# Gate and up of a pair of expert tiles: seven block products, with partial sums kept in PSUM, in place of eight

## The chip, the cores and the metric

The kernel runs on one core of a Trainium2 chip. The metric is the device time of one execution in microseconds (us), as the median of the runs shown. All data are float32 unless a line says otherwise. The engines are named as in the profile: PE is TensorE (PEld its weight loads), DVE is VectorE, ACT is ScalarE, POOL is GpSimd, and SP issues most DMAs. P is 128, D is 512, KC (the number of 128-row chunks of D) is 4.

## What is computed

The reference is a decoder of two layers over 16 sequences of 128 tokens: a state space scan, cross attention, a ternary feed forward, self attention, gated cross attention, and last a mixture of experts. The change touches only the last, which for a token x reads (cut):

```python
scores = softmax(x @ gate_w.T)                 # 64 experts in 8 groups of 8
topk_w, topk_idx = top_k(scores, 8)
flat = w_e[:, inv_map]; scalar = flat.sum(-1)  # weight of each group
soft = softmax(where(flat == 0, -1e9, flat))
xg = x[:, None, :] + einsum('ngi,ghi->ngh', soft, mask_up_w)
g = einsum('ngh,gih->ngi', xg, gate_proj_w)    # 352 x 512 for each group
u = einsum('ngh,gih->ngi', xg, up_proj_w)
a = silu(g) * u
d = einsum('ngi,ghi->ngh', a, down_proj_w)
y = einsum('ng,ngh->nh', scalar, d)
```

## The kernel before

The stages run one after the other; `stage_moe` is the last, from about 2150 us of the profiled span to its end. A token is copied into the bucket of each group that it needs, and the groups then work on tiles of 128 tokens. The work list `units` holds 53 units, 40 of two tiles ("pairs") and 13 of one. It goes through the eight groups twice: first the first five tiles of each group (two pairs and a single), then the later ones (mostly three pairs); near the end four `beyond` units for overfull buckets stand between the groups, and the last pair takes its tokens from `placed`. Each of the 16 passes (`q`) has its weights: `gu`, 128 x 4 x 704, which holds in its columns 256 rows of gate, 256 of up, and the remaining 96 of gate and 96 of up; and `dn` for down.

The loop in `stage_moe` is a software pipeline written out by hand. In step t it does, for PE, in this order: `rest` (L2010) of unit t, the 96 + 96 left-over columns with the tokens as stationary operand, into PSUM tile `pr`; `gate` (L2035), 8 matmuls into `pg`, and after them the transposes of the left-over activations (`pta`, L2041); `up` (L2045), 8 matmuls into `pu`; then `places` of unit t+2 (transposes, `pts`, L1985); `turn_in` of unit t+1, which makes that unit's token block `xgT` (soft times mask-up plus the transposed row, PSUM tiles `px`, copied out by ACT at L2007 and DVE at L2007); and last `down` of unit t (`y`, L2063), whose results DVE scales (`yo`, L2080) and ACT's queue stores (L2081). A float32 matmul of the source appears as two records of the profile, so 8 matmuls are "x16".

The element work between them: ACT takes silu of `pr` (L2020) and DVE multiplies it with the up part (L2021) before `pta` can start; ACT copies `pta` to `aT` (L2043); ACT takes silu of `pg` (L2038), DVE multiplies `pu` into it (L2047), and both `aT` and `act` are read by `down`.

PSUM has eight banks: `pg`, `pu` and `pr` have one tile each (pool `s6g`), the pool `s6p` has three tiles that all of `pta`, `pts` and the two `px` take in turn, and `y` has two. The matmuls of `gate`, `up`, `down`, `places` and `turn_in` are kept in program order; the order of everything else on each engine's queue is the tile scheduler's. Each engine runs its own queue in order.

`half()` in each step also moves other work along: the routing of the last eight token blocks (`route`, L1691, in the first nine steps or so; its exponentials change ACT's function table, which silu changes back), the gathers of finished results (`got`, L2086), POOL's additions of them to x (L2098), and layer norms.

Of the kernel before, what the change touches and what calls it, by code (L numbers as in the profile page):

```python
# [10 lines left out]
F32 = mybir.dt.float32  # L11
# [4 lines left out]
AF = mybir.ActivationFunctionType  # L16
ALU = mybir.AluOpType
# [3 lines left out]
P = 128  # L21
NB = 16
D = 512
KC = D // P
# [1573 lines left out]
class Moe:  # L1598
# [330 lines left out]
    def pair(self, g, j, n):  # L1929

        u, k = Ctx(), self.k
        u.g, u.j, u.n, u.s = g, j, n, None
# [6 lines left out]
    def placed(self, g, b, n):  # L1939

        u = Ctx()
        u.g, u.n, u.b, u.to, u.s = g, n, b, None, None
        u.src = [self.k.rows[b + i][:, :].unsqueeze(1) for i in range(n)]
        return u

    def beyond(self, s):

        u = Ctx()
        u.s, u.n, u.to = s, 1, [self.k.over_results[s][1:, :]]
        return u  # L1950

    def fetch(self, u):
# [7 lines left out]

    def open(self):

        self.wk = self.k.moe_ctx.enter_context(self.k.tc.tile_pool(name="s6o", bufs=1, side="right"))
        self.depth = 1
        self.opened = u = self.pair(0, 0, 2)
        self.fetch(u)
        yield
        yield
        self.places(u)
        yield  # L1970
        yield from self.turn_in(u)
# [17 lines left out]
    def turn_in(self, u, keep=lambda ins: ins):  # L1989

        nc, n, mup = self.nc, u.n, self.mup[u.g] if u.s is None else self.over_mup[u.s]
        u.xT = self.wk.tile([P, KC, 2, P], F32, tag="xgT", name="xgT")
        pxs = [self.pp.tile([P, 2, 2, P], F32, tag="pp", name="px") for _ in range(2)]
        cols = [slice(c * P, (c + 1) * P) for c in range(KC)]
        for c, at in enumerate(cols):
            keep(nc.tensor.matmul(
                pxs[c // 2][:, c % 2, 0:n], mup[:, at], u.soft[:, 0:n], start=c % 2 == 0, stop=False, skip_group_check=True
            ))
        for h, px in enumerate(pxs):
            for e in range(2):  # L2000
                for i in range(n):
                    keep(nc.tensor.matmul(
                        px[:, e, i], u.row[:, i, cols[2 * h + e]], self.k.ident, is_transpose=True,
                        start=False, stop=e == 1 and i == n - 1, skip_group_check=True,
                    ))
            copy = nc.vector.tensor_copy if h else nc.scalar.copy
            copy(u.xT[:, 2 * h : 2 * h + 2, 0:n], px[:, :, 0:n])  # L2007
            yield

    def rest(self, u):  # L2010

        nc, n, R, (gu, _) = self.nc, u.n, self.I - 2 * P, u.w
        pr = self.pgu.tile([P, 2, 2 * R], F32, tag="pr", name="pr")
        for i in range(n):
            for c in range(KC):
                nc.tensor.matmul(pr[:, i], u.xT[:, c, i], gu[:, c, 4 * P :], start=c == 0, stop=c == KC - 1)  # L2016
        u.rest = self.rests[0]
        self.rests.reverse()
        r = u.rest[:, 0:n, 0:R]
        nc.scalar.activation(r, pr[:, 0:n, 0:R], AF.Silu)  # L2020
        nc.vector.tensor_tensor(r, pr[:, 0:n, R:], r, ALU.mult)  # L2021

    def whole(self, u, lo, tag):

        n, (gu, _) = u.n, u.w
        ps = self.pgu.tile([P, 2, 2, P], F32, tag=tag, name=tag)
        for e in range(2):
            for c in range(KC):
                at = lo + e * P
                self.k.tc.keep_in_program_order(  # L2030
                    self.nc.tensor.matmul(ps[:, e, 0:n], gu[:, c, at : at + P], u.xT[:, c, 0:n], start=c == 0, stop=c == KC - 1)  # L2031
                )
        return ps[:, :, 0:n]

    def gate(self, u):  # L2035
        pg = self.whole(u, 0, "pg")
        u.aT = self.wk.tile([P, 2, 2, P], F32, tag="act", name="act")
        self.nc.scalar.activation(u.aT[:, :, 0 : u.n], pg, AF.Silu)  # L2038
        pt = self.pp.tile([P, 2, P], F32, tag="pp", name="pta")
        for i in range(u.n):  # L2040
            self.k.tc.keep_in_program_order(self.nc.tensor.transpose(pt[:, i], u.rest[:, i], self.k.ident))  # L2041
        u.rT = self.wk.tile([P, 2, P], F32, tag="aT", name="aT")
        self.nc.scalar.copy(u.rT[:, 0 : u.n], pt[:, 0 : u.n])  # L2043
# [112 lines left out]
def stage_moe(k):  # L2156
# [4 lines left out]
    with ExitStack() as ctx:  # L2161
# [120 lines left out]
        with tc.If(over > 0):  # L2282
            for b in range(NB):
                nc.sync.dma_start(k.x[b], k.rows[b][:, 0:D])
            for g in range(NG):
                w = m.load(wp, g)
                for b in range(0, NB, 2):
                    u = m.placed(g, b, 2)
                    u.w = w
                    m.fetch(u)  # L2290
                    m.places(u)
# [147 lines left out]
```

## Time and profile before

| what | value |
|---|---|
| three runs | 2970.22, 2973.87, 2977.48 us (median 2973.87) |
| the profiled execution | 2971.48 us, of which the span of its trace 2969.5 us |
| from 2150 to 2970 us of the span (820 us) | PE busy 797.0, PEld 616.8, DVE 252.1, ACT 152.4, POOL 426.5 us |
| all POOL additions of gathered results (L2098) | 134 x 1.27 us |
| all DVE multiplications after up (L2047) | 40 of 128 x 512 at 0.691 us, 13 of 128 x 256 at 0.423 us |
| granted TensorE clock, mean of the execution | 0.991 |

A row of a timeline gives start, duration, engine, source line, operation, output from inputs, shape and count; several like instructions are merged into one row. The duration of a PE row runs to the modelled end of its last matmul; the time that PE spends on a row is read from its start to the start of the next one.

### The profile page before, as it was taken

To read this page: it belongs to the slowest core of one execution; us is meant where nothing else is said; L and a number is where in the kernel's file an instruction comes from. 1 tells how busy PE (TensorE), PEld (TensorE's weight loads), DVE (VectorE), ACT (ScalarE), POOL (GpSimd) and SP (SyncE) were. 2 spreads that over 40 slices of the span, in tenths; PEclk is the share of its full clock that TensorE was granted. 3 is DMA by queue.
4 is the path that set the end of the run, shared out by engine and by line. 5 is a ranking of instruction groups with operands and counts; after the bars stand their busy time and mean duration, and the time that the engine had idled before them with its cause. 6 is when DMAs were issued, how large, how long until landed. Compare 5 with 4: busy or idle time off the path is not lost.

```text
span 2969.5 us, 41833 instructions
## 1 busy us (share of the span) xinstructions
PE 2868.5 (97%) x14422; PEld 1929.5 (65%) x14446; DVE 1887.1 (64%) x4263; ACT 1326.2 (45%) x3265; POOL 1562.8 (53%) x1352
## 2 busy tenths in 40 slices
PE   7999999999999999999999999999999999999998
PEld 6666665555555555555787656566577777777776
DVE  6999997766766676755897798667743321332224
ACT  6887884333343333336434698655632211111111
POOL 7999996434333333431333474246646564335555
PEclk9999999999999999999999999999999999999999
DMA  6755454780000000005000200224267776555664
GB/s 201 217 138 128 130 134 124 261 301 15 8 8 15 8 8 15 8 29 159 27 1 1 72 2 1 61 87 150 95 223 250 249 240 203 172 190 169 203 206 145
DMA packets 177393, 345.24 MB, mean 116 GB/s; under 512 B 25277, under 2 KB 84157, under 8 KB 175638
## 3 DMA queue, kind: packets, MB, share of 16 engines
q1 hardware_dynamic: 126342, 217.64, 24.4%
q0 software_dynamic: 26016, 80.80, 8.1%
q10 hardware_dynamic: 24816, 44.05, 4.0%
q8 instruction: 116, 1.90, 0.3%
q14 instruction: 103, 0.84, 0.1%
HBM read 256.22 MB, written 151.99 MB: 137 GB/s over the span
## 4 chain that ended last, share of the span: by engine, by line
PE 65%; DVE 13%; ACT 3%; issue 1%; POOL 1%; DMA 1%; SPq 0%; ACTq 0%; DVEq 0%; POOLq 0%
PE y L2063 8%; PE pq L708 7%; PE po L828 6%; PE pu L2031 5%; PE pg L2031 5%; PE pr L2016 4%; PE po L1040 4%; PE ao L817 3%; PE sc L777 3%; PE pt L568 2%; PE pg L1020 2%; PE pT L805 2%; PE pu L1020 2%; PE pk L708 1%; PE pw L1514 1%
## 5 line engine op out<-in xcount | busy, mean ns | idle before, releaser
L797 POOL TENSOR_TENSOR pr<-pr,sm 128x512 f32<-128x512 f32 x128 | 135.3, 1057 | 366.2 <-DVE sm L796 276.5
L66 POOL TENSOR_TENSOR dBx<-dtx,BC 128x1024 f32<-128x1024 f32 (+1 forms) x131 | 300.5, 2316 | 16.0 <-DVE h L66 9.4
L790 ACT ACTIVATE pr<-sc,mx,sf 128x256 f32<-128x256 f32 x256 | 142.3, 560 | 335.7 <-DVE mx L783 299.7
L66 ACT ACTIVATE h<-dt,negA 128x254 f32<-128x254 f32 x512 | 244.1, 477 | 16.8 <-ACT h L66 0.2
L2086 POOL DMA_INDIRECT got<-results,gidx x126 | 121.1, 961 | 215.6 <-DMA results<-yo 184.6
L828 PE MATMUL po<-w,aT 128*128 128x512 f32 x512 | 233.1, 593 | 1.0 <-DVE aT L822 1.0
L708 PE MATMUL pq<-w,xT 128*128 128x512 f32 x512 | 231.4, 595 | 0.0
L2098 POOL TENSOR_TENSOR x<-got,x 128x512 f32<-128x512 f32 x134 | 168.2, 1272 | 89.0 <-DMA got<-results,gidx 86.1
L679 POOL TENSOR_TENSOR m<-m,m 128x512 f32<-128x512 f32 x96 | 122.6, 1277 | 116.6 <-DVE m L674 113.3
L66 DVE TENSOR_TENSOR_SCAN h<-h,dBx 128x1024 f32<-128x1024 f32 x72 | 164.9, 2290 | 27.1 <-ACT h L66 21.5
L2047 DVE TENSOR_TENSOR act<-pu,act 128x512 f32<-128x512 f32 (+1 forms) x53 | 33.1, 625 | 230.5 <-PE pu L2031 209.2
L2063 PE MATMUL y<-dn,act 128*128 128x512 f32 x372 | 175.2, 593 | 1.5 <-DVE act L2047 1.5
L2031 PE MATMUL pu<-xgT,gu 128*128 128x256 f32 (+1 forms) x848 | 172.2, 357 | 0.0
L2031 PE MATMUL pg<-xgT,gu 128*128 128x256 f32 (+1 forms) x848 | 170.0, 354 | 0.0
L66 PE MATMUL pkv<-w,cT 128*128 128x512 f32 x368 | 167.5, 598 | 1.1 <-DMA w<-in_x_wvT 1.1
L1030 POOL TENSOR_TENSOR lo<-sg,hi 128x512 fp32r<-128x512 f32 x64 | 84.1, 1314 | 156.5 <-ACT hi L1029 156.4
L2080 DVE TENSOR_SCALAR yo<-y,row 128x512 f32<-128x512 f32 x87 | 65.3, 751 | 155.0 <-PE y L2063 153.2
L708 PEld LDWEIGHTS pq<-w,xT 128*128 128x128 f32 x512 | 94.6, 191 | 101.0 <-issue 93.3
L828 PEld LDWEIGHTS po<-w,aT 128*128 128x128 f32 x512 | 94.7, 190 | 100.9 <-issue 97.0
L1830 POOL DMA_INDIRECT bucket<-r_row,r_to x126 | 124.8, 990 | 58.8 <-issue 35.7
L2031 PEld LDWEIGHTS pg<-xgT,gu 128*128 128x128 f32 x848 | 145.5, 191 | 14.4
L2031 PEld LDWEIGHTS pu<-xgT,gu 128*128 128x128 f32 x848 | 144.1, 192 | 15.0
(462 smaller groups left out, 6962.4 us busy)
## 6 DMA issues: line engine op xcount, KB each, us to landing
bucket<-zeros SPq DMA_DIRECT2D x88, 388.0 KB, 9.1
BC<-bcd SPq DMA_DIRECT2D x128, 256.0 KB, 5.4
row<-bucket SPq DMA_DIRECT2D x39, 776.0 KB, 5.3
gu<-in_moe_guT SPq DMA_DIRECT2D x16, 1408.0 KB, 7.8
results<-yo ACTq DMA_DIRECT2D x87, 256.0 KB, 4.5
x_k<-kv ACTq DMA_DIRECT2D x32, 256.0 KB, 4.2
x_v<-kv ACTq DMA_DIRECT2D x32, 256.0 KB, 5.1
v<-x_v SPq DMA_DIRECT2D x32, 256.0 KB, 2.6
```

What stands on the lines that cost most here:

```text
L66: return self.tc.keep_in_program_order(call(*args, **kw))
L679: nc.gpsimd.tensor_tensor(m1, m1, m2, ALU.add)
L708: nc.tensor.matmul(ps, src[:, c], w[c], start=c == 0, stop=c == KC - 1)
L790: nc.scalar.activation(pr[:, j], st.sc[g, i][:, j], AF.Exp, scale=st.sf[:, h : h + 1], bias=st.mx[g, i][:, j : j + 1], accum_out=sm[:, j : ...
L797: nc.gpsimd.tensor_tensor(pr, pr, sm.unsqueeze(2).to_broadcast([P, 2, 2 * P]), ALU.mult)
L828: nc.tensor.matmul(st.po, aT[:, j], k.wo[h // 8][:, h % 8], start=h == 0, stop=h == G * J - 1)
L1020: nc.tensor.matmul(p[:, e], w[:, c, at : at + P], sn.qT[:, :, c], start=c == 0, stop=c == KC - 1)
L1830: return self.nc.gpsimd.indirect_dma_start(out=table[:, :], out_offset=bass.IndirectOffsetOnAxis(ap=to[:, i, g : g + 1], axis=0), in_=row[ ...
L2031: self.nc.tensor.matmul(ps[:, e, 0:n], gu[:, c, at : at + P], u.xT[:, c, 0:n], start=c == 0, stop=c == KC - 1)
L2063: self.k.tc.keep_in_program_order(self.nc.tensor.matmul(y, aT, dn[:, c], start=c == 2, stop=c == 1))
L2086: self.nc.gpsimd.indirect_dma_start(out=got[:, :], out_offset=None, in_=table, in_offset=bass.IndirectOffsetOnAxis(ap=at, axis=0),)
L2098: self.nc.gpsimd.tensor_tensor(self.k.x[b], got, self.k.x[b], ALU.add)
```

## The change

For every pair except the first one of the stage (and except the overflow path, which is not taken with these inputs), gate and up together are taken as one product of 2 x 2 blocks. The left matrix has gate and up (256 rows each) as its block rows and the two halves of D as its block columns; the right matrix has the halves of D as block rows and the two tiles of tokens as block columns. The eight block products become seven, by Strassen's scheme in Winograd's form. A block product is 4 matmuls of 128 x 128 by 128 columns (two row blocks, two chunks of D).

- `weight_sums` makes four sums of weight blocks for each pass, 128 x 512 each, on DVE; three live in the slot of the tile `row` of an older pool, the fourth in a tile of its own.
- `differences` makes four differences of token blocks, 128 x 256 each, on DVE, after the copies of `turn_in`.
- `split_gate` runs products 1, 2, 5, 6, 3 before `rest`; product 7 stands inside `rest`, between the matmuls of the first and the second tile; product 4 stands in `split_last`, where `up` was.
- Partial sums stay in PSUM: product 6 is added on top of product 1 (`u.q`, in the tile `pu`), 7 and 4 on top of that, product 3 on top of product 5 (in the tile `pg`). Between two products ACT copies the value that is needed at that point (L2055, L2058, L2059), and DVE adds (L2060, L2062, L2069) and multiplies (L2070, L2074).
- silu of the 512 gate columns reads SBUF (L2063) instead of PSUM.
- The transposes `pta` move from behind `gate` to behind product 4 (`turn_rest`).
- `xgT` has one buffer instead of two.

```diff
     def turn_in(self, u, keep=lambda ins: ins):
-        u.xT = self.wk.tile([P, KC, 2, P], F32, tag="xgT", name="xgT")
+        u.xT = self.wk.tile([P, KC, 2, P], F32, tag="xgT", name="xgT", bufs=1)
...
+        if u.split:
+            self.differences(u)
+
+    def weight_sums(self, pool, gu):
+        nc = self.nc
+        (a11, a12), (a21, a22) = [[gu[:, 2 * h : 2 * h + 2, r : r + 2 * P] for h in range(2)] for r in (0, 2 * P)]
+        s4 = pool.tile([P, 2, 2 * P], F32, tag="sums", name="sums", bufs=1)
+        s = self.left.tile([P, 2, self.ROW], F32, tag="row", name="sums3").rearrange("p a b -> p (a b)")
+        s1, s2, s3 = (s[:, 4 * P * i : 4 * P * (i + 1)].rearrange("p (c r) -> p c r", c=2) for i in range(3))
+        for to, x, y, op in (
+            (s1, a21, a22, ALU.add), (s2, s1, a11, ALU.subtract), (s3, a11, a21, ALU.subtract), (s4, a12, s2, ALU.subtract)
+        ):
+            nc.vector.tensor_tensor(to, x, y, op)
+        return a11, a12, s4, a22, s1, s2, s3
+
+    def differences(self, u):
+        (b11, b12), (b21, b22) = [[u.xT[:, 2 * h : 2 * h + 2, i] for i in range(2)] for h in range(2)]
+        t = self.left.tile([P, KC, 2, P], F32, tag="xgT", name="diff")
+        for i, (x, y) in enumerate(((b12, b11), (b22, t[:, 0]), (b22, b12), (b21, t[:, 1]))):
+            self.nc.vector.tensor_tensor(t[:, i], x, y, ALU.subtract)
+        u.right = b11, b21, b22, t[:, 3], t[:, 0], t[:, 1], t[:, 2]
+
+    def seventh(self, u, n, ps, start=False):
+        w, x = u.w[2][n - 1], u.right[n - 1]
+        for e in range(2):
+            for c in range(2):
+                self.k.tc.keep_in_program_order(self.nc.tensor.matmul(
+                    ps[:, e], w[:, c, e * P : (e + 1) * P], x[:, c], start=start and e == 0 and c == 0, stop=c == 1,
+                    skip_group_check=True,
+                ))
+
+    def split_gate(self, u):
+        nc = self.nc
+        gate = self.pgu.tile([P, 2, 2, P], F32, tag="pg", name="pg")
+        u.q = self.pgu.tile([P, 2, 2, P], F32, tag="pu", name="pu")[:, 0]
+        x, r = gate[:, 0], gate[:, 1]
+        u.fifth = self.wk.tile([P, 2, P], F32, tag="fifth", name="fifth", bufs=1)
+        u.aT = self.wk.tile([P, 2, 2, P], F32, tag="act", name="act")
+        a, b = u.aT[:, :, 0], u.aT[:, :, 1]
+        self.seventh(u, 1, u.q, start=True)
+        self.seventh(u, 2, x, start=True)
+        nc.scalar.copy(a, u.q)
+        self.seventh(u, 5, r)
+        self.seventh(u, 6, u.q)
+        nc.scalar.copy(u.fifth, r)
+        nc.scalar.copy(b, u.q)
+        nc.vector.tensor_tensor(a, x, a, ALU.add)
+        self.seventh(u, 3, r)
+        nc.vector.tensor_tensor(b, r, b, ALU.add)
+        nc.scalar.activation(u.aT, u.aT, AF.Silu)
+
+    def split_up(self, u):
+        nc = self.nc
+        self.seventh(u, 7, u.q)
+        nc.vector.tensor_tensor(u.fifth, u.q, u.fifth, ALU.add)
+        nc.vector.tensor_tensor(u.aT[:, :, 1], u.fifth, u.aT[:, :, 1], ALU.mult)
+
+    def split_last(self, u):
+        self.seventh(u, 4, u.q)
+        self.nc.vector.tensor_tensor(u.aT[:, :, 0], u.q, u.aT[:, :, 0], ALU.mult)
...
     def rest(self, u):
...
+            if u.split and not i:
+                self.split_up(u)
...
@@ stage_moe, step t @@
-                m.rest(u)
-                m.gate(u)
+                if u.split:
+                    m.split_gate(u)
+                    m.rest(u)
+                else:
+                    m.rest(u)
+                    m.gate(u)
             half()
             m.tick()
             if u:
-                m.up(u)
+                if u.split:
+                    m.split_last(u)
+                    m.turn_rest(u)
+                else:
+                    m.up(u)
+            if t + 1 in first and t > 0:
+                q = first[t + 1]
+                weights[q] = *weights[q], m.weight_sums(wp, weights[q][0])
...
             if u:
                 m.down(u)
                 m.store(u)
+            if t == 0:
+                weights[0] = *weights[0], m.weight_sums(wp, weights[0][0])
```

More of the change, by code (lines that the diff above doesn't have):

```diff
@@ L1931, in pair @@
         u, k = Ctx(), self.k
-        u.g, u.j, u.n, u.s = g, j, n, None
+        u.g, u.j, u.n, u.s, u.split = g, j, n, None, n == 2
         late = j >= self.FIRST
@@ L1937, in pair, with placed @@
         return u
-    def placed(self, g, b, n):
+    def placed(self, g, b, n, split=True):
         u = Ctx()
-        u.g, u.n, u.b, u.to, u.s = g, n, b, None, None
+        u.g, u.n, u.b, u.to, u.s, u.split = g, n, b, None, None, split
         u.src = [self.k.rows[b + i][:, :].unsqueeze(1) for i in range(n)]
@@ L1948, in beyond @@
         u = Ctx()
-        u.s, u.n, u.to = s, 1, [self.k.over_results[s][1:, :]]
+        u.s, u.n, u.split, u.to = s, 1, False, [self.k.over_results[s][1:, :]]
         return u
@@ L1961, in open @@
     def open(self):
-        self.wk = self.k.moe_ctx.enter_context(self.k.tc.tile_pool(name="s6o", bufs=1, side="right"))
+        self.wk = self.left = self.k.moe_ctx.enter_context(self.k.tc.tile_pool(name="s6o", bufs=1, side="right"))
         self.depth = 1
         self.opened = u = self.pair(0, 0, 2)
+        u.split = False
         self.fetch(u)
@@ L2010, in rest @@
+    def split_up(self, u):
[6 more added lines that the diff above has]
+        self.nc.vector.tensor_tensor(u.aT[:, :, 0], u.q, u.aT[:, :, 0], ALU.mult)
     def rest(self, u):
-        nc, n, R, (gu, _) = self.nc, u.n, self.I - 2 * P, u.w
+        nc, n, R, gu = self.nc, u.n, self.I - 2 * P, u.w[0]
@@ L2015, in rest @@
             for c in range(KC):
-                nc.tensor.matmul(pr[:, i], u.xT[:, c, i], gu[:, c, 4 * P :], start=c == 0, stop=c == KC - 1)
+                self.k.tc.keep_in_program_order(
+                    nc.tensor.matmul(pr[:, i], u.xT[:, c, i], gu[:, c, 4 * P :], start=c == 0, stop=c == KC - 1)
+                )
+            if u.split and not i:
+                self.split_up(u)
         u.rest = self.rests[0]
@@ L2023, in whole @@
     def whole(self, u, lo, tag):
-        n, (gu, _) = u.n, u.w
+        n, gu = u.n, u.w[0]
         ps = self.pgu.tile([P, 2, 2, P], F32, tag=tag, name=tag)
@@ L2038, in gate, with turn_rest @@
         self.nc.scalar.activation(u.aT[:, :, 0 : u.n], pg, AF.Silu)
+        self.turn_rest(u)
+    def turn_rest(self, u):
         pt = self.pp.tile([P, 2, P], F32, tag="pp", name="pta")
@@ L2287, in stage_moe @@
                 for b in range(0, NB, 2):
-                    u = m.placed(g, b, 2)
+                    u = m.placed(g, b, 2, split=False)
                     u.w = w
```

## The prediction

> **What bounds the kernel now.** First the page's busy times and its chain of waits, then the busy times by stretch of the expert stage, then the timeline of one pair.
>
> ```profile
> PE 2868.5 (97%) x14422; PEld 1929.5 (65%) x14446; DVE 1887.1 (64%) x4263; ACT 1326.2 (45%) x3265; POOL 1562.8 (53%) x1352
> ...
> PE 65%; DVE 13%; ACT 3%; issue 1%; POOL 1%; DMA 1%; SPq 0%; ACTq 0%; DVEq 0%; POOLq 0%
> ...
> 2400.00:2560.00 160.00, 160.00 (x790) 125.00 (x790) 31.50 (x52) 21.73 (x56) 73.79 (x70) 1.00 0.59 193
> ```
>
> From 2400 to 2560 us PE is busy for all of 160 us, at clock 1.00, while DVE works 31.5 and ACT 21.7. What leaves PE's queue shortens the stage; what DVE or ACT gets costs nothing until PE waits for it. PE in one pair:
>
> ```profile
> 2566.75 2.76 PE L2016 MATMUL pr<-gu,xgT 128*128 128x192 f32 x16
> 2569.35 3.62 PE L2031 MATMUL pg<-xgT,gu 128*128 128x256 f32 x16
> 2572.80 0.38 PE L2041 MATMUL pta<-ident,rest 128*128 128x128 f32 x2
> 2573.02 3.62 PE L2031 MATMUL pu<-xgT,gu 128*128 128x256 f32 x16
> 2576.48 0.38 PE L1985 MATMUL pts<-ident,row 128*128 128x128 f32 x2
> 2576.61 0.72 PE L1996 MATMUL px<-soft,mup 128*128 128x256 f32 x4
> 2577.17 1.04 PE L2002 MATMUL px<-ident,row 128*128 128x128 f32 x8
> 2578.04 1.02 PE L2063 MATMUL y<-dn,aT 128*128 128x512 f32 x2
> ...
> 2583.20 2.11 PE L2016 MATMUL pr<-gu,xgT 128*128 128x192 f32 x12
> ```
>
> From start to start: 16.45 us for the pair, of it 2.60 `pr`, 3.45 `pg`, 3.46 `pu`, 0.22 `pta`, 0.13 `pts`, 0.56 + 0.87 `px`, 5.16 `y`, and no gap. The elementwise work hides because each result has 3.45 us of other matmuls before PE needs it:
>
> ```profile
> 2569.55 0.33 ACT L2020 ACTIVATE rest<-pr 128x192 f32<-128x192 f32 x1 [7.55 <-PE pr L2016]
> 2569.91 0.36 DVE L2021 TENSOR_TENSOR rest<-pr,rest 128x192 f32<-128x192 f32 x1 [2.21 <-ACT rest L2020]
> ```
>
> `rest` is done at 2570.27 and `pta` wants it at 2572.80. These rows also give hops: PE's row ends at 2569.35, ACT begins 0.20 later; ACT to DVE 0.03.
>
> **The saving.** 32 records of 256 columns (6.91 us) become 56 of 128 columns. Units of one tile show what such a record costs:
>
> ```profile
> 2253.07 1.95 PE L2031 MATMUL pu<-xgT,gu 128*128 128x128 f32 x16
> 2254.86 0.38 PE L1985 MATMUL pts<-ident,row 128*128 128x128 f32 x2
> ```
>
> 16 in 1.79 us, 0.112 each, so 56 take 6.27 and a pair saves 0.64: an eighth off, less 3.6% for the smaller matmuls. 40 pairs less the first are 39: -25.0 us.
>
> **The new waits in each pair.** Two places come too close. The remaining hops are in a unit where `pta` already waited:
>
> ```profile
> 2219.23 0.35 DVE L2021 TENSOR_TENSOR rest<-pr,rest 128x192 f32<-128x192 f32 x1
> 2219.64 0.44 PE L2041 MATMUL pta<-ident,rest 128*128 128x128 f32 x2 [0.20 <-DVE rest L2021]
> 2219.91 0.60 PE L568 MATMUL pt<-ident,x 128*128 128x128 f32 x4
> 2220.17 0.37 ACT L2043 COPY aT<-pta 128x256 f32<-128x256 f32 x1
> ```
>
> DVE to PE 0.06; a waiting transpose pair takes 0.27 instead of 0.22, as its weights are no longer loaded ahead; `pta` to its copy 0.53. A `y` chain that waited at 2226.85 took 1.82 us against 1.72: 0.10 for the same reason.
>
> Product 3. In the built order of the changed program the addition x + a (L2060) waits for ACT's copy of product 5 (one signal is given after products 2 and 5), and product 3, which writes the same PSUM tile, waits for that addition. From the end of product 5: 0.20, copy of 256 columns 0.37 (L2043 row), 0.03, addition 0.42 (mean of the 128 x 256 `act` rows), 0.06, weight load 0.10 = 1.18. Only product 6 covers it, 8 x 0.112 = 0.90. Lost 0.28; 39 pairs +10.9. Behind the waiting matmul stands all of PE's queue.
>
> `pta` and the second `px`. After the last `pr` matmul stands only product 4. Silu and multiply need 0.20 + 0.33 + 0.03 + 0.36 + 0.06 = 0.98, with 0.05 for the load, against 0.90: lost 0.13. And four tiles (`pta`, `pts`, two `px`) go through three PSUM buffers, so the second `px` waits for ACT's copy of `pta`: 0.53 + 0.37 + 0.06 = 0.96 from the start of `pta`, against 0.27 + 0.13 + 0.28 = 0.68 of cover; with 0.04 for the load, lost 0.32. Before, `pu` hid this copy. Together 0.45, 39 times: +17.6.
>
> So waits of 0.73 meet a saving of 0.64. Bounds of the 0.73: 0.54 without the three load terms, 0.94 if ACT's three hops from PE are 0.27, as DVE's (`pts` at 2576.48, L2047 at 2576.75).
>
> **Weight sums.** Four DVE additions for each of 16 passes, 0.69 each (L1672, 128 x 512, both inputs in SBUF). In the built order 15 of the 16 sets have two of them in DVE's queue between the addition after product 7 (L2069) and the multiplication that `pta` waits for (L2091). From the end of product 7: 0.27 + 0.42, then 0.69, 0.42 (L2070) and 0.69 with gaps of 0.03, then 0.36: done at 2.97. Without them `pr` (1.30) and silu decide: 1.30 + 0.20 + 0.33 + 0.03 + 0.36 = 2.22. Late by 0.75, after PE already waits: 15 times, +11.3. Bounds: 0 if the scheduler's order didn't matter, 1.5 if both are held up as long again. The first set falls into the second unit and is counted below.
>
> **Token differences** at nothing: from the end of `px`, 0.27 + 0.69 copy + 4 x 0.41 + gaps is 2.7 us, beneath `down` and products 1 and 2 (5.16 + 1.79). Uncovered they would cost 39 x 2.7 = 105. Two copies more on ACT and a silu from SBUF: beneath products and `pr`. One `xgT` buffer at nothing: its last reader, product 4, precedes the next write on PE's own queue. No DMA is added or moved.
>
> **Routing, in the first nine changed pairs.** Here DVE's queue holds strings of small operations between the additions that PE now waits for: 17 before L2060 of the second pair (some 3.7 us after `yo`, done 1.4 late), 14 in the seventh (1.2), 12 and 21 around L2062 of the ninth (about 3), and in the first pair the four sums and three operations of the routing (2.5). The trace shows such a unit with cover only. I take +8, bounds 3 and 15.
>
> **POOL.** The changed DVE operations with both inputs in SBUF meet POOL's additions:
>
> ```profile
> 2630.44 8.61 POOL L2098 TENSOR_TENSOR x<-got,x 128x512 f32<-128x512 f32 x7
> ...
> 2634.66 4.95 DVE L1925 TENSOR_TENSOR mup_raw<-mup_raw,mup_over 128x512 f32<-128x512 f32 x1 [1.17 <-ACT mup_over L1924]
> ```
>
> L1925 takes 0.69 three times of four; here it ends 0.56 after POOL's seventh addition. The multiplication L2070 has 0.72 us of slack (1.14 against 1.86 after product 7), so one addition of 1.27 seldom hurts; but runs that last from 5.0 to 12.4 us after a unit's start (2796.13, unit at 2791.10) or from 4.4 to 11.8 (2853.44, at 2849.07) would hold it from 7.7 to the run's end, with some 4 us lost each, and the L1925 above would now stand before L2060. Two or three such events: +8; bounds 0, if the runs shift, and 20.
>
> The Trainium skill (SBUF — State Buffer, Who interferes with whom) has DVE and GpSimd hold the shared port for one instruction. By that L1925 would have waited for the end of one addition, 1.27 at most, and this term would be about 1; the row waited through four, so the row decides.
>
> **Sum.** -25.0 + 10.9 + 17.6 + 11.3 + 8 + 8 = +30.8. The profiled execution took 2971.48 (span 2969.5), so 3002.3; the median shown is 2.4 higher: 3005.
>
> **Rivals.**
>
> A, the other side: the products stay dense, because PE's weight loads run ahead and the copies come in time. The 160 of 160 us speaks for PE's queue as the only limit; the waits in the built order speak against it. It decides if a pair's waits stay under 0.64 - 11.3/39 = 0.35 us. With none, and the sums in full: 2973.9 - 25.0 + 11.3 = 2960. Chance 0.08.
>
> B: the pair's waits as worked out, but sums, routing and POOL mostly hidden: -25.0 + 28.5 + about 2 = +5, 2979. For it: PE lost under 5 us to DVE in the routing units before (2.9 at `pta`, 1.5 at `y`, 0.4 at `px`). Against: the cover has gone from 3.45 us to 0.9. Chance 0.11.
>
> C: the DVE and POOL port becomes the bound. L672 with SBUF inputs beside a busy POOL averages 1.30 us against 0.69 for the same shape from PSUM. Sums at 1.30: 15 x 1.2 = +18 more; the eight long POOL runs (5 to 8.6 us) at 4 each, 32 in place of 8. +31 + 18 + 24 = +73: 3047. Against: the runs near 2580 to 2730 end 5 to 6.5 us into a unit, before L2070. Chance 0.11.
>
> The forecast, 0.70.
>
> **How the numbers follow.** 3005 is the likeliest case. Its own bounds: low, 0.54 a pair, half of the sums, 3 and 0: -25.0 + 21.1 + 5.6 + 3 = +5; high, 0.94 a pair, 1.5 a set of sums, 15 and 20: -25.0 + 36.7 + 22.5 + 15 + 20 = +69. All ends together are unlikely, so I take 2983 to 3030, leaving A and most of B out below, most of C above. 0.2% is about 6 us, what a measurement of this kernel can tell from no change. Faster 0.08 (A), same 0.08 (the larger part of B), slower 0.84.
>
> **What would show it.** Right: gate and up take 6.3 us of PE's time in a pair; gaps before product 3 (about 0.3, from DVE L2060), `pta` (L2091) and the second `px` (ACT's copy), some 0.7 in all; 15 pairs with 0.7 more at `pta`. A pair without gaps would make it wrong to the fast side; L2031 or L2070 rows of several us in many pairs, or product 5 waiting for the differences, to the slow side. Steady pairs of about 16.5 us, against 16.45, decide between the forecast and A.

## The result, and the profile after

The changed kernel takes 3021.56 us (median of four runs, 3018.04 to 3028.11) against 2972.32 for the kernel before on the same chip: 1.0166 times as long, 95% interval 1.0143 to 1.0188. It is slower by 49 us. (Four of the kernels below ran on a chip on which the kernel before itself took 3036 us; in the four traces from it engines stand still, up to 10.7 us at a time, with nothing that the profile shows to wait for, so these four are read unit by unit.) The profiled execution has a span of 3016.3 us, 46.8 more than before. Busy times, and the head of the chain of waits, from the page of the changed kernel:

```profile
PE 2877.0 (95%) x15382; PEld 1953.1 (65%) x15382; DVE 2071.3 (69%) x4639; ACT 1371.3 (45%) x3382; POOL 1572.8 (52%) x1352
...
PE 62%; DVE 15%; ACT 3%; DMA 2%; issue 2%; POOL 1%; SPq 0%; ACTq 0%; DVEq 0%; POOLq 0%
```

DVE has 184 us more than before, and its share of the chain grew from 13% to 15%. PE is not busy for less time, although an eighth of gate and up is gone. But this view counts short waits between matmuls as busy, as the steady pair below shows. The stretch that before held 160 us of PE's work, by busy times (length, then PE, PEld, DVE, ACT, POOL, granted clock, DMA share, GB/s):

```profile
2400.00:2560.00 160.00, 158.13 (x971) 126.31 (x971) 68.13 (x132) 30.79 (x79) 77.00 (x70) 1.00 0.60 198
```

A steady pair, in the timeline of PE:

```profile
2546.96 1.06 PE L2039 MATMUL pu<-diff,sums 128*128 128x128 f32 x8
2548.05 1.16 PE L2039 MATMUL pg<-xgT,sums 128*128 128x128 f32 x8
2549.04 1.47 PE L2083 MATMUL pr<-gu,xgT 128*128 128x192 f32 x8
...
2552.54 1.05 PE L2039 MATMUL pu<-diff,gu 128*128 128x128 f32 x8
2553.51 0.44 PE L2114 MATMUL pta<-ident,rest 128*128 128x128 f32 x2
2553.79 0.38 PE L1986 MATMUL pts<-ident,row 128*128 128x128 f32 x2
2553.93 1.00 PE L1997 MATMUL px<-soft,mup 128*128 128x256 f32 x4
2554.77 1.03 PE L2003 MATMUL px<-ident,row 128*128 128x128 f32 x8
```

These rows are, from the top, product 6, product 3, the left-over matmuls of the first tile, then product 4, `pta`, `pts` and the two kinds of `px` rows. From start to start, product 6 takes 1.09 instead of 0.89 and product 3 0.99 (a wait of 0.20 for x + a, then a weight load that was not made ahead); product 4 takes 0.97 and `pta` 0.28 instead of 0.22; the first `px` rows take 0.84 instead of 0.56. That is 0.72 us of waiting, though PE counts as busy for 16.47 of the pair's 16.51 us. Before, the pair took 16.45.

Where 46.4 us went by the start of the last unit's `down` can be read from the starts of the `y` rows of all 53 units, each unit's time (from the `y` of the unit before to its own) beside that before:

| where | us more than before |
|---|---|
| ahead of unit 0's `y` | 5.1 |
| units 1 to 25 together | 5.4 |
| units 28, 31, 41, 45 | 9.8 + 4.4 + 4.4 + 4.7 = 23.3 |
| the other units after 25 | 12.6, mostly 1.0 to 1.6 in each of the seven pairs with weight sums; 3.9 in units 36, 48, 51 and 52; 0.06 in an ordinary pair |

Half of the loss sits in four units. The worst, unit 28, by the timelines of DVE, POOL, ACT and PE:

```profile
2592.15 9.09 DVE L90 SCALAR_TENSOR_TENSOR rs_t<-rs_t,rs_a 128x2 f32<-128x2 f32 x1
...
2603.55 0.74 DVE L2153 TENSOR_SCALAR yo<-y,row 128x512 f32<-128x512 f32 x1
...
2592.64 8.58 POOL L2171 TENSOR_TENSOR x<-got,x 128x512 f32<-128x512 f32 x7
...
2602.37 2.35 ACTq L2154 DMA_DIRECT2D results<-yo  x2
2604.76 0.37 ACT L2055 COPY act<-pu 128x256 f32<-128x256 f32 x1 [14.69 <-DMA results<-yo]
...
2605.18 2.07 PE L2039 MATMUL pu<-diff,sums 128*128 128x128 f32 x8 [7.52 <-ACT act L2055]
2607.05 1.92 PE L2039 MATMUL pg<-xgT,sums 128*128 128x128 f32 x8
```

A layer norm operation on 128 x 2 elements, 0.16 us elsewhere, takes 9.09: it starts at 2592.15 and ends at 2601.24, with POOL's seventh addition (2601.22). Behind it on DVE stands `yo`; the store that waits for `yo` stands on ACT's queue ahead of the copy of product 1; product 6 overwrites what that copy reads, and waits 7.52. Below, such a row, many times as long as the same operation takes elsewhere, is called held. In unit 31 it is L1925 (4.61 us, then product 3 waits 3.90 for the addition behind it); in units 41 and 45 the multiplication L2070 (4.29 and 4.74), and `pta` waits for what stands behind that. First unit 31, then unit 41 with POOL's run beside it:

```profile
2657.54 4.61 DVE L1925 TENSOR_TENSOR mup_raw<-mup_raw,mup_over 128x512 f32<-128x512 f32 x1 [1.17 <-ACT mup_over L1924]
...
2663.05 2.07 PE L2039 MATMUL pg<-xgT,sums 128*128 128x128 f32 x8 [3.90 <-DVE act L2060]
...
2830.68 4.29 DVE L2070 TENSOR_TENSOR act<-fifth,act 128x256 f32<-128x256 f32 x1
2834.90 0.34 DVE L2091 TENSOR_TENSOR rest<-pr,rest 128x192 f32<-128x192 f32 x1
...
2827.32 7.37 POOL L2171 TENSOR_TENSOR x<-got,x 128x512 f32<-128x512 f32 x6
```

### The profile page after: what moved, and what is told of

It reads as the page before. It is cut to its first block, busy times and chain, and to the rows that moved or that the text cites. A ratio compares the mean times of both kernels' runs of the same rounds, so it can differ in the third digit from the quotient of the medians.

```text
span 3016.3 us, 44189 instructions
## 1 busy us (share of the span) xinstructions
PE 2877.0 (95%) x15382; PEld 1953.1 (65%) x15382; DVE 2071.3 (69%) x4639; ACT 1371.3 (45%) x3382; POOL 1572.8 (52%) x1352
## 4 chain that ended last, share of the span: by engine, by line
PE 62%; DVE 15%; ACT 3%; DMA 2%; issue 2%; POOL 1%; SPq 0%; ACTq 0%; DVEq 0%; POOLq 0%
PE y L2136 7%; PE pq L708 7%; PE po L828 6%; PE po L1040 4%; PE pu L2039 4%; PE pg L2039 3%; PE pr L2083 3%; PE ao L817 3%; PE sc L777 3%; PE pt L568 2%; PE pg L1020 2%; PE pu L1020 2%; PE pT L805 1%; PE ps L1429 1%; PE pw L1514 1%
## 5 line engine op out<-in xcount | busy, mean ns | idle before, releaser
L66 POOL TENSOR_TENSOR hs<-hs,BC 128x1024 f32<-128x1024 f32 x56 | 132.1, 2359 | 23.1 <-DVE hs L66 23.1
L1483 ACT ACTIVATE at_s<-sc,mx,r 128x128 f32<-128x128 f32 x256 | 114.7, 467 | 60.2 <-DVE mx L1475 55.7
L2083 PE MATMUL pr<-gu,xgT 128*128 128x192 f32 x744 | 139.5, 332 | 0.0
L66 DVE TENSOR_TENSOR_SCAN hs<-h,dBx 128x1024 f32<-128x1024 f32 x56 | 127.8, 2284 | 12.5 <-PE py L66 10.7
L777 PE MATMUL sc<-kT,qT 128*128 128x256 f32 x512 | 131.8, 380 | 0.0
L2136 PEld LDWEIGHTS y<-dn,act 128*128 128x128 f32 x372 | 70.7, 190 | 90.9 <-issue 86.1
```

The source lines that it names most:

```text
L66: return self.tc.keep_in_program_order(call(*args, **kw))
L777: nc.tensor.matmul(sc[:, j], st.qT[g][:, 2 * i + j], st.kT[:, g], start=True, stop=True)
L2136: self.k.tc.keep_in_program_order(self.nc.tensor.matmul(y, aT, dn[:, c], start=c == 2, stop=c == 1))
```

## The experiments

Twelve kernels in three lots, each lot beside runs of the kernel before on its own chip. Ratios are against those runs. The second lot, of four, is the one on the disturbed chip.

### The left-over matmuls of dense units unpinned

The change also keeps the left-over matmuls (`rest`) of every unit in program order on PE's queue, called pinned here; before, the scheduler could place them. This takes the pin from the units that keep dense products:

```diff
-                self.k.tc.keep_in_program_order(
-                    nc.tensor.matmul(pr[:, i], u.xT[:, c, i], gu[:, c, 4 * P :], ...)
-                )
+                mm = nc.tensor.matmul(pr[:, i], u.xT[:, c, i], gu[:, c, 4 * P :], ...)
+                if u.split:
+                    self.k.tc.keep_in_program_order(mm)
```

> The left-over matmuls of units that keep their dense products may again be placed by the scheduler; only those of split pairs stay pinned in program order. Theory (a step that the prediction missed): in the changed kernel the first unit's `pr` matmuls stand on PE's queue behind the `pts` that waits for a row until 2168.9 us, so that 6.9 us stand empty there and unit 0's `down` starts at 2183.3 instead of 2178.2. Unpinned, unit 0 gets its 5.1 us back (`down` at about 2178.2) and the whole takes about 3016.5 (5 below 3021.6). Rival (the weight sums or the routing delay unit 0): `down` of unit 0 stays near 2183 and the time at 3021.

Measured: 1.0171 (1.0151 to 1.0190). Unit 0's `y` starts at 2179.0, as expected; the wait for the row is 3.4 us instead of 6.9 (3.2 in the kernel before, 6.9 to 7.6 in all five kernels with these matmuls pinned on undisturbed chips). But by unit 13 the delay is 6.0 us (9.4 in the changed kernel), and the total is the same within its interval. So the pinned matmuls explain 3.5 us of wait ahead of unit 0; the start of its `y` also scatters by some 3 us from trace to trace (2.7 to 5.7 us late in the five pinned kernels, and 2.9 early in the kernel before with broken-up runs, below). What is won there is mostly lost again behind it.

### The weight sums behind the differences

```diff
-            nc.vector.tensor_tensor(to, x, y, op)
+            self.k.tc.keep_in_program_order(nc.vector.tensor_tensor(to, x, y, op))
...
@@ stage_moe @@
-            if t + 1 in first and t > 0:
-                q = first[t + 1]
-                weights[q] = *weights[q], m.weight_sums(wp, weights[q][0])
             if t + 2 > 0 and unit(t + 2):
                 m.places(units[t + 2], tc.keep_in_program_order)
             if t + 1 > 0 and unit(t + 1):
                 for _ in m.turn_in(units[t + 1], tc.keep_in_program_order):
                     pass
+            if t + 1 in first and t > 0:
+                q = first[t + 1]
+                weights[q] = *weights[q], m.weight_sums(wp, weights[q][0])
```

> The changed kernel with the four weight sums of a pass pinned on DVE's queue behind the token differences of the next unit; nothing else is changed. Theory (order on DVE's queue): the 14 waits of `pta` for the multiplication behind the sums (18.3 us in all) shrink to the 0.1 of an ordinary pair, and PE gains 11 (15 sets at 0.75) to 17 us: 3005 to 3011. Rival (the sums' 2.8 us each cost wherever they stand, because products 5 and 6 then wait for them): pg or pu wait for L2023 instead, and the time stays within 4 us of 3021.6.

Measured: 1.0196 (1.0164 to 1.0228), so no gain. The later pairs with sums do lose their wait (unit 26 takes 16.50 instead of 17.53, unit 32 16.50 instead of 17.50; 6.9 us in the seven pairs with sums after unit 25, and 1.3 in units 16, 19 and 22), and products wait only 0.6 us for the sums. The total does not fall, because everything behind has moved against POOL's additions, and a token difference is now held twice, which costs unit 37 8.7 us and unit 31 2.4 more. DVE's timeline:

```profile
2650.78 9.79 DVE L2031 TENSOR_TENSOR diff<-xgT,diff 128x256 f32<-128x256 f32 x2
...
2759.68 9.82 DVE L2031 TENSOR_TENSOR diff<-xgT,diff 128x256 f32<-128x256 f32 x2
```

### Another order on PE

```diff
@@ split_gate @@
         nc.vector.tensor_tensor(a, x, a, ALU.add)
-        self.seventh(u, 3, r)
-        nc.vector.tensor_tensor(b, r, b, ALU.add)
-        nc.scalar.activation(u.aT, u.aT, AF.Silu)
+        u.third = r, b
@@ split_up @@
+        nc, (r, b) = self.nc, u.third
+        self.seventh(u, 3, r)
+        nc.vector.tensor_tensor(b, r, b, ALU.add)
+        nc.scalar.activation(u.aT, u.aT, AF.Silu)
         self.seventh(u, 7, u.q)
@@ down @@
-            for c, aT in ((2, u.rT[:, i]), (0, u.aT[:, 0, i]), (1, u.aT[:, 1, i])):
...
+            parts = [(0, u.aT[:, 0, i]), (1, u.aT[:, 1, i])]
+            parts.insert(2 * u.split, (2, u.rT[:, i]))
@@ stage_moe @@
                     m.split_last(u)
-                    m.turn_rest(u)
...
             if u:
+                if u.split:
+                    m.turn_rest(u)
                 m.down(u)
```

> The seven products with another order on PE: product 3 behind the left-over matmuls of the first tile, `pta` behind both `px`, and `down` taking the 256 rows of `act` first and `aT` last. Sums, differences and all element work as in the changed kernel. Theory (the cost is the uncovered waits, not the work): a steady pair falls from 16.51 to 16.45 - 0.64 = 15.8 us, the waits before product 3, `pta` and `px` go to nothing and the sums no longer hold `pta`; 39 x 0.7 + 11 = about 38 us less than 3021.6, 2983, and less again by what POOL's long runs no longer reach: 2965 to 2985. Rival (the smaller matmuls do not run at 0.112 us in a chain, or DVE's added work is the limit): steady pairs stay above 16.2 and the time above 3005.

Measured: 2994.47 us, 1.0093 (1.0075 to 1.0110). The steady pair is as expected; its busy times:

```profile
2541.74:2557.53 15.79, 15.79 (x102) 12.82 (x100) 8.23 (x16) 3.41 (x9) 4.34 (x5) 1.00 0.42 122
```

15.79 us, with PE never idle and DVE at work for 8.2 of it: 0.66 less than 16.45, and nothing in the work itself forbids the saving. The total misses its range because the held operations stay: units 28, 31, 37, 41, 42, 45 and 46 lose 31 us against before (10.3 and 7.7 in units 28 and 37), while the 25 units that are faster by 0.3 or more gain 16.1.

### Dense products, the new work on DVE kept

```diff
-                if u.split:
-                    m.split_gate(u)
-                    m.rest(u)
-                else:
-                    m.rest(u)
-                    m.gate(u)
+                m.rest(u)
+                m.gate(u)
...
-                if u.split:
-                    m.split_last(u)
-                    m.turn_rest(u)
-                else:
-                    m.up(u)
+                m.up(u)
```

> All units take gate and up by the eight dense products, `pta` behind `pg` and `pu` behind it, as before the change; the weight sums and token differences are still computed on DVE but not used, and `xgT` has one buffer. Theory (added DVE work is hidden where PE's cover is as before): a steady pair at 16.45, the time 2972 to 2982 (5 of it from the pinned left-over matmuls of unit 0). Rival (DVE's work and its port shared with POOL bind by themselves): 2995 or more, with `down` or products waiting for L2031 or L2023.

Measured: 2993.26 us, 1.0092 (1.0072 to 1.0112): between the two expectations. From unit 16 on a pair takes 15.95 or 16.45 as before, sums and differences and all; unit 31 loses 3.5 (L1925 is held 6.80 us), and two units of one tile 0.6 each. But 16.2 us are gone by unit 15, 5.7 ahead of unit 0 (the pinned matmuls) and the rest where DVE also carries the routing. PE's waits there, from 2160 to 2430 us:

```profile
PE pta L2112 <- DVE rest L2089: 8.4, 5, 2.5
PE pts L1986 <- DMA row<-bucket: 7.0, 1, 7.0
```

So the added DVE work is hidden in the steady part and not in the routing part, even behind dense products. (This kernel has the single `xgT` buffer too; the waits, nearly all for DVE, speak against it as the cause, but it was not tried alone.)

### POOL's additions left out, in the changed kernel and in the one before

```diff
     def add(self, b, got):
-        self.nc.gpsimd.tensor_tensor(self.k.x[b], got, self.k.x[b], ALU.add)
+        pass
```

> The changed kernel without POOL's 134 additions of gathered results to x (left out, so x lacks the experts' results; gathers, layer norms and stores stay). Theory (a DVE instruction with two SBUF inputs is held while POOL works through a run of additions): the rows of 9.1, 4.6, 4.3 and 4.7 us on DVE fall to their own 0.16 to 0.7, units 28, 31, 41 and 45 lose their 10, 4.4, 4.4 and 4.6 us, and the time falls by about 23 to 2998. Rival (DVE waits there for something else, or PE's slow matmuls after the waits have a cause of their own): units 28 to 45 keep their delays and the time stays above 3012.

> The kernel before without POOL's 134 additions of gathered results to x (left out in the same way). Theory: with eight dense products PE has the cover, so holding DVE costs next to nothing there; only the 1.9 us of unit 31 (L1925 held 4.95) can go: 2968 to 2973. Rival (the additions slow the kernel before as well, by the shared port): more than 10 us faster, below 2960.

Measured, on the disturbed chip: 1.0181 (1.0152 to 1.0211) and 1.0082 (1.0061 to 1.0102). The totals decide nothing, as the stalls decide them; PE's longest waits in the first trace end with instructions that DVE and ACT began late for no shown reason (groups of DVE's waits, total, times, longest):

```profile
DVE act L2060 <- issue: 21.9, 4, 8.4
```

The units do decide. Without additions no DVE row after 2200 us is longer than 2 us. Units 28, 31, 41 and 45 take 17.49, 18.14, 16.50 and 16.50 against 26.29, 22.77, 20.88 and 21.09 in the changed kernel: 22.4 us less. In the kernel before units 25 to 39 stay as they were, but for unit 31's 1.9 us (16.45 instead of 18.36). What POOL's additions cost the one kernel and not the other is shown by these units; that the kernel as a whole gets faster by it is not shown by this pair.

### All edits of order together, then POOL's runs broken up

The three edits of order above (dense units unpinned, sums behind the differences, the other order on PE), and the multiplication's operand in PSUM:

```diff
-        u.q = self.pgu.tile([P, 2, 2, P], F32, tag="pu", name="pu")[:, 0]
+        pu = self.pgu.tile([P, 2, 2, P], F32, tag="pu", name="pu")
+        u.q, u.sum = pu[:, 0], pu[:, 1]
...
-        nc.vector.tensor_tensor(u.fifth, u.q, u.fifth, ALU.add)
-        nc.vector.tensor_tensor(u.aT[:, :, 1], u.fifth, u.aT[:, :, 1], ALU.mult)
+        nc.vector.tensor_tensor(u.sum, u.q, u.fifth, ALU.add)
+        nc.vector.tensor_tensor(u.aT[:, :, 1], u.sum, u.aT[:, :, 1], ALU.mult)
```

> The new order on PE (product 3 behind the left-over matmuls of the first tile, `pta` behind `px`, `act` before `aT` in `down`), the weight sums pinned behind the token differences, the sum after product 7 written to the free half of the PSUM tile `pu` so that the multiplication L2070 reads PSUM, and the left-over matmuls pinned in split pairs alone. Theory: from the 2994.5 of the new order, the two L2070 rows held 6.3 and 5.5 us (about 8 us of PE) and the sums held behind `pta` (units 42 and 46, 4.4 us) go: about 2982, with the layer norm row, L1925 and L2031 still held at POOL's long runs; 2965 to 2990 as these shift. Rival (reading PSUM doesn't help, or sums now hold products 3 and 5): 2994 or more.

And on top of it:

```diff
+    def combine_run(self, g, bs):
+        keep, got = self.k.tc.keep_in_program_order, []
+        yield
+        for n in range(len(bs) + 2):
+            if n < len(bs):
+                got.append(self.result(g, bs[n], keep))
+            if n >= 2:
+                keep(self.add(bs[n - 2], got[n - 2]))
...
+            if j == T - 1 and u.g < NG - 1:
+                running.append(m.combine_run(u.g, list(range(j, end))))
+                return
             for b in range(j, end):
                 running.append(m.combine(u.g, b))
```

> As the run before, and POOL's runs of six or seven back-to-back additions broken up: gather and addition alternate on POOL's queue, two gathers ahead, for the second pass of groups 0 to 6. Nothing is left out. Theory (a DVE instruction is held until POOL's run of additions ends, so short runs hold it briefly): no DVE row above 4 us, units 28, 31, 37 lose most of their 10, 4.5 and 8.4 us, 20 less than the run before: 2955 to 2968, below the kernel before. Rival (the total of POOL's additions counts, not the length of a run): within 5 us of the run before.

Measured, on the disturbed chip: 1.0129 (1.0091 to 1.0167) and 0.9958 (0.9942 to 0.9975). With its operand in PSUM the multiplication is held nowhere, but six of the long runs now catch a token difference (rows of 5.3 to 9.8 us), and one the layer norm. Breaking up the runs gives 59 us between the medians, but not all of that is due to the runs. Units 31, 34 and 37, in which a difference was held for 9.0 to 9.4 us, gain 27.6 (unit 37 takes 15.80 instead of 24.95). Units 40, 44 and 48 gain another 31.2, yet no DVE row in them is held in the slower kernel (in unit 40 DVE stands idle for 10.7 us ahead of an addition of 0.42), and on the same chip they take 26.7 to 29.4 us in the changed kernel without any additions: that is the disturbance. Unit 28 gains 0.8. So in three units the length of POOL's runs seems to count, not the number of additions; the next pair tests that on an undisturbed chip.

### The runs broken up, and nothing else; the same in the kernel before

The last diff alone, put into the changed kernel and into the kernel before.

> The changed kernel with only one thing altered: on POOL's queue gathers and additions alternate, two gathers ahead, for the second pass of groups 0 to 6, so that runs of six or seven back-to-back additions (7.4 to 8.6 us) become single ones or pairs (1.3 to 2.5 us) with a gather's issue between. Theory (a DVE instruction that meets POOL's additions is held to the end of their run): no DVE row above 4 us, units 31, 41 and 45 lose their 4.4 us each, unit 28 part of its 10 (several shorter holds remain there): 12 to 20 us less, 3002 to 3010 against 3021.6, or 1.010 to 1.013 of the kernel before. Rival (the number of additions counts, not the length of the run): 1.0166 as the changed kernel.

> The kernel before with the same alternation of gathers and additions on POOL's queue, eight dense products. Theory: with the cover of dense products holds on DVE cost it only the 1.9 us of unit 31, so 0.999 to 1.001 of the kernel before. Rival (the alternation is a gain by itself, whatever the products are): below 0.995.

Measured: 3005.85 us, 1.0118 (1.0102 to 1.0133), and 1.0000 (0.9990 to 1.0009). The first is 14 us better than the changed kernel by the ratios, in the range expected; the second shows that dense products have nothing to win there. So the run length is a cause by itself. No DVE row is longer than 3.4 us, and units 41 and 45 are back at 16.50. Units 28 and 31 gain only 0.5 each (25.74 and 22.27), which was not expected. In unit 31 L1925 is still held, for 3.38 us, and product 3 waits 2.89. Unit 28's DVE and POOL:

```profile
2590.43 1.70 DVE L89 TENSOR_TENSOR rs_t<-rs_y 128x2 f32<-128x2 f32 x1
...
2592.79 1.83 DVE L91 SCALAR_TENSOR_TENSOR rs_y<-rs_t,rs_y 128x2 f32<-128x2 f32 x1
...
2590.83 1.27 POOL L2171 TENSOR_TENSOR x<-got,x 128x512 f32<-128x512 f32 x1
2592.26 1.04 POOL L2159 DMA_INDIRECT got<-results,gidx  x1 [0.16 <-POOL x L2171]
2593.33 1.27 POOL L2171 TENSOR_TENSOR x<-got,x 128x512 f32<-128x512 f32 x1
```

Small operations of the layer norm now each meet an addition, and these two are let go when theirs ends (2592.13 against 2592.10, 2594.62 against 2594.60). Five such holds, of 1.2 to 3.0 us, add up to 9.4 us: several short ones delay `yo` nearly as much as one long hold did.

### The stores moved to SP's queue, and the additions moved to DVE

On top of the version with broken-up runs:

```diff
-            nc.scalar.dma_start(u.to[i], yo)
+            nc.sync.dma_start(u.to[i], yo)
```

> The version with the new order on PE, sums behind the differences, L2070's operand in PSUM and POOL's alternation, and the results `yo` stored from SP's queue in place of ACT's. Theory (in unit 28 the held layer norm delays `yo`, the store waiting for `yo` stands in ACT's queue ahead of the copy of product 1, and product 6 waits for that copy): unit 28 falls from 26.3 us to under 19, the rest as without the stores moved: steady pairs 15.8, the whole 0.985 to 0.992 of the kernel before. Rival (product 6 waits for ACT for another reason): unit 28 stays at 24 or more.

Measured: 2970.59 us, 0.9999 (0.9990 to 1.0008): all edits together bring the seven products level with the eight, no further. Unit 28 takes 24.1 us, as the rival had it. ACT is free now, but DVE's own queue behind the held layer norm is late for x + a, and product 3 waits for that:

```profile
2586.21 2.08 PE L2039 MATMUL pg<-xgT,sums 128*128 128x128 f32 x8 [5.34 <-DVE act L2061]
```

So the store on ACT's queue was where the delay passed, not its cause. Against the kernel before with broken-up runs, on the same chip, 30 units gain 19.4 us together, 23 of them 0.63 to 0.66 each; units 1, 3, 13, 28, 31, 36 and 48 lose 22.3, of which unit 28 has 7.7, 48 has 4.9 (three weight sums of 2.1 to 2.3 us, each held by a single addition, and products 5 and 6 wait for them) and 13 has 4.5 (3.3 of it because product 4 waits for L2072, which reads the other half of the same PSUM tile: a wait that the edit itself brought).

```diff
-        self.nc.gpsimd.tensor_tensor(self.k.x[b], got, self.k.x[b], ALU.add)
+        self.nc.vector.tensor_tensor(self.k.x[b], got, self.k.x[b], ALU.add)
```

The additions moved, and spread over half steps in place of the alternation:

> As the run before, but the 134 additions of gathered results are made by DVE (one or two for each half step, so no long row of them) and none by POOL; nothing is left out. Theory (DVE was held by POOL's additions, while it has room for work as such): no DVE row above 2 us after 2200, unit 28 under 17.5, 134 x 0.7 = 94 us more on DVE hidden, 0.983 to 0.990 of the kernel before, at or below the run before. Rival (DVE's amount of work is what binds, as rival C of the prediction has it): steady pairs with an addition take longer by 0.5 us or more, and the time is at or above the kernel before.

Measured: 3130.10 us, 1.0533 (1.0518 to 1.0549). No DVE row after 2200 us is longer than 2 us, so the holds are gone. But DVE takes its queue in order, and an addition that waits for its gather stops all that stands behind. DVE's waits, then PE's:

```profile
DVE x L2175 <- DMA got<-results,gidx: 172.5, 76, 9.7
...
PE pu L2039 <- DVE act L2072: 111.9, 36, 10.3
```

The rival's time came true without its reason: DVE did not run out of time (from 2200 to 3130 us it is busy for 438 of 930 us), it stood waiting for DMAs.

## Why the prediction came out as it did

The direction and the mechanism (uncovered waits eat the saving, and POOL's runs hold DVE) were right, and 3021.6 lies within 2983 to 3030. The point, 3005, was 16.6 us too low. Step by step:

- The saving of 0.64 in a pair is right. It shows once the waits are taken away: 15.79 us in the other order, and 0.63 to 0.66 in each of 23 units of the kernel with the stores moved.
- The new waits in each pair are right: 0.30 at product 3 (forecast 0.28), 0.14 at `pta` (0.13), 0.28 at `px` (0.32); 0.72 in all against 0.73. The steady pair of 16.51 decides for the forecast and against rival A.
- The weight sums were forecast at +11.3 as 15 times 0.75. Moving them gave back about 8: near 1.0 in each of seven later pairs, where the first sums of a set meet one of POOL's additions (from 2540 us on sums<-gu averages 1.34 us against 0.68), and 0.2 to 0.8 in three early ones. Size about right, spread wrongly.
- Routing was forecast at +8. The delay by unit 13 is 9.4, but 5.1 of it arises ahead of unit 0, 3.5 of that from a step that the prediction did not list: `rest` is pinned on PE's queue by the change, and stands behind a wait for a DMA. Unpinned, the delay by unit 13 is 6.0, of it 0.8 ahead of unit 0.
- "Token differences at nothing" holds in the steady part (dense products with all the new DVE work: 16.45), not in the routing part, where that kernel lost 10.5 behind unit 0 (all of DVE's new work together).
- POOL was the term mis-sized: +8 forecast, with bounds of 0 and 20, and 22 to 23 measured. "Two or three such events" were four. Those that were named came as named, L2070 held by the two runs of six (units 41 and 45) and L1925 ahead of L2060 (unit 31), 13.5 us together; they alone cost more than the 8. The one that was not named cost most, 9.8: a layer norm operation of 128 x 2, in the kernel all along. The prediction's list held the changed instructions and L1925, and did not ask what else on DVE's queue might now meet a run. In the kernel before, this layer norm stands behind `rest` of unit 27 (2569.91, shown in the prediction) and was over before POOL's run began:

```profile
2574.08 1.00 DVE L105 TENSOR_SCALAR x<-x,ln_mv,rs_y 128x512 f32<-128x512 f32 x2
...
2580.59 8.62 POOL L2098 TENSOR_TENSOR x<-got,x 128x512 f32<-128x512 f32 x7
```

- In the changed kernel it stands behind `rest` of unit 27 again, but that now comes behind the products, 5.9 us later against the units, and token differences run between its steps; so L90 meets the run at its start. Old instructions were exposed in two ways: they moved in time, and the cover shrank. That the cover counts shows in unit 31: L1925, held 4.95 us, cost 1.9 in the kernel before, and, held 4.61, cost 4.6 in the changed one (22.77 against 18.14 without additions; the kernel before, 18.36 against 16.45). Dense products cover some of a hold and not any length of it: with them and the new DVE work, L1925 held 6.80 makes unit 31 take 21.90 against the 16.45 of the kernel before without additions. Whether they would have hidden a hold of 9 us, no run shows.
- The sum of +30.8 against 46.4: 15 of the missing 16 is this one term. That the others, forecast at 22.8 together, came to 23.1 is partly luck: the sums (about 8 for 11.3) and the routing behind unit 0 (4.3 for 8) were forecast too high, and the 5.1 ahead of unit 0 and 3.9 in units 36, 48, 51 and 52 were not forecast at all.
- Rival B's "2.9 at `pta`" in the routing units is a misreading: 1.7 of it lies in unit 31, behind the held L1925, so the kernel before already paid for one of POOL's runs.
- Rival C priced POOL's runs at 32 and doubled the sums. The first half of it was nearer than the forecast's term; the second was true of some of the sums only (1.34 and 0.68 us, above).
- Weighing rule against row, the prediction followed the row, rightly. The Trainium skill (SBUF — State Buffer, Who interferes with whom) has whichever of the two issues first hold the shared port for its whole instruction, while the other side blocks. Here an operation that began 0.49 us before the first of seven back-to-back additions ended with the last (9.09 us), and with a gather's issue behind the addition such an operation was let go after one (1.70 and 1.83 us). That is not without exception: in the kernel with only the runs broken up, L90 was let go between the second and the third of three back-to-back additions (2.99 us).

## What to carry to other kernels

When a change shortens the busiest engine's work by splitting it, list what the removed length was covering, for every instruction on the queues that now come due, also the old ones, and see whether these have moved in time. A saving of 0.64 us in a pair is gone if the dependent chain has 0.9 us of cover where it needs 1.2; reordering got it back, where adding up engine loads would have shown nothing. On a queue served in order look for the rare event (a run of another engine's additions, a gather), not only for the mean.

## What the runs showed that was not expected

A DVE operation with a single SBUF input can be held as well: L86, a TENSOR_SCALAR on 128 x 2, took 1.73 us beside POOL's pair of additions in the kernel with only the runs broken up, 2.93 in the one with dense products, and 0.17 in the changed kernel. The rows that ran in the gaps took their usual time (with only the runs broken up, a difference 0.41 at 2592.05, while POOL's queue went from an addition to a gather's issue).

After the long waits here PE runs at half its rate for some microseconds, which adds to each event: behind the 7.52 us wait of unit 28 eight matmuls take 1.87 us instead of 0.89 from start to start, and the granted clock (the third number from the end) is

```profile
2605.20:2608.00 2.80, 2.80 (x13) 2.80 (x14) 0.42 (x1) 0.57 (x2) 0.00 (x0) 0.50 0.98 242
2608.00:2611.00 3.00, 3.00 (x16) 3.00 (x16) 0.42 (x1) 0.63 (x1) 0.95 (x1) 0.67 0.42 166
2611.00:2614.00 3.00, 3.00 (x24) 2.89 (x23) 1.42 (x4) 0.33 (x1) 0.96 (x2) 1.00 0.52 172
```

0.50, then 0.67, then 1.00. The Trainium skill (TensorE: Matmul & The Clock Gate, Part 1) states such a halving after an idle window of some 3.4 us, and full rate after as long a busy one; the rows agree, with half rate behind a wait of 7.52 us and full rate from 2611 us at the latest, 6 us after the restart, but they do not measure the window. At these clocks 2.80 us at 0.50 and 3.00 us at 0.67 lose 1.4 + 1.0 = 2.4 us, which with the wait makes up the 9.8 us that unit 28 lost.

What stays open: the cause of the idle stretches on the chip of the second lot, and whether a version with the layer norm moved out of POOL's way would beat the kernel before. The 0.9958 was measured on that chip alone, where idle stretches move single units by 10 us and more, and on another one the same edits with the stores moved came to 0.9999; so no version here is shown to be faster than the kernel before.
